# Layer 1's last stage in a four-layer graph network: four chunks' attention on ScalarE, the last softmax inside an output, scatters in five and three, x in twos

## The chip, the core and the metric

The kernel runs on one core of a Trainium2 chip. The core has five engines that work side by side, each with its own queue: TensorE (PE) for matrix products, VectorE (DVE), ScalarE (ACT), GpSimd (POOL), and SyncE (SP), which here only starts transfers. The metric is the device time of one launch in microseconds (us). The time before is 2069.36 us, the median of three runs (2069.28 to 2069.97).

## The reference

The input x has 128 x 64 = 8192 tokens of 256 numbers. Four layers follow each other, each of the form "normalize, cut off below zero, apply a graph network, add to x":

```python
h = jnp.maximum(_layernorm(x, axis=-1), 0.0)
x = x + _L1_gnn_ref(h, W_lin, W_val, a, W_out, adj, src, dst)
```

The change lies in layer 1, an attention over 512 edges of a graph with 64 nodes and 4 heads:

```python
Xq = (H @ W_lin.T).reshape(bt, n, h, dh);  Xv = (H @ W_val.T).reshape(bt, n, h, dh)
e = jnp.einsum('behd,hd->beh', leaky_relu(Xq[:, src] + Xq[:, dst], 0.2), a)
e = e + jnp.log(A0[src, dst] + EPS)[None, :, None]
# softmax of e over the edges with the same src gives attn
Y = segment_sum(attn[..., None] * Xv[:, dst], src)      # weighted sum of the values
return Y @ W_out.T
```

Layer 0 (products with the adjacency matrix and four LSTMs), layer 2 (two dense layers with batch norms) and layer 3 (a dense attention) are not touched. All numbers are 32-bit floats.

## The kernel before

**Chunks and groups.** Layer 1 works on 16 chunks of 512 tokens (NCH) and on 4 groups of 4 chunks. The edges of a group are scored together. Its softmax turns the scores into attention numbers for the 512 edges; these are scattered into a field in HBM that has a place for every pair of nodes (zero where there is no edge), and the field is read back as one dense tile `dense[g]` of 2 MB. From then on a chunk's weighted sum is a set of small dense products.

**A chunk's last steps.** `fetch(n)` (L1107) starts two transfers of 0.5 MB on SP: the values `xv` (chunks 12 to 15 still have theirs in SBUF) and the residual `x`, into a buffer of the pool `xo` (4 buffers), or, for chunks 13 to 15, into buffers that are no longer used. `turn_attention(n)` (L1126) copies the chunk's part of the dense tile into the order that PE needs, in two halves: `o = 0` on ACT, `o = 1` on DVE, both L1132, into a tile of the pool `attc` (3 buffers). `weigh(n)` (L1139) does the weighted sum: 32 small products, 64 matmul instructions in the trace (L1150), and a copy of the result to `yT` on ACT (L1160; 2 buffers). `put_out(n)` (L1165) multiplies by W_out in two halves of 8 matmul instructions each (L1171) and adds each half to x on DVE (L1181). Then x goes back to HBM (L1247 on SP), and `sums(n)` (L1185) takes mean and root of the variance for the next layer's norm: four pairs of `bn_stats` and `bn_aggr` on DVE (L1190, L1191), four small operations on POOL (L1193 to L1198). The tiles between DVE and POOL have 4 buffers.

**The order of a step.** `values_of(n)` (L1220) is a chunk's turn. It weighs chunk n, fetches chunk n + 2, turns the attention of chunk n + 2 (chunk 12, `LAST`, the first of the last group, is turned at the end of chunk 11's turn, and chunk 13 in chunk 12's), stores what was added a turn ago, puts out chunk n - 1, and then does some of the sums that are due. With `hold` the sums are put off. Chunks 0 to 3 have their turns between the edges of the last group; chunks 4 to 15 follow in the loop at L1328.

**The softmax of a group.** `edge_softmax(g)` (L1012) is a generator: each `yield` is a place at which other work is traced. `step_behind()` runs it to its next `yield`, `finish_behind()` to its end. It goes through an addition, four scans along the edges, a subtraction, an exponential on ACT (L1025), four reciprocals and a product that gives `e` (L1037), all but the exponential on DVE; then four transposes on PE (L1043), for the last group four scalings on ACT that give `attn` (L1051), eight indirect transfers from POOL (L1072, "scatters") and the read-back (L1093), which waits for all eight. POOL works its queue in order, so what is behind the read-back in it waits as well. For the last group (g = 3) the first four steps are taken after the last edges, the next seven in chunk 4's turn, the transposes and `attn` ahead of chunk 6's weighing. The scatters then go out in groups, each of which also waits for the last weighing traced before it (`last_weigh`, "weights first"):

```python
if len(sent) in (3, 6):
    yield
```

so three after chunk 6's weighing, three after chunk 7's, two and the read-back after chunk 8's.

**What sets the order on an engine.** A planner orders each engine's instructions by a simulation at build time. `late(ins)` pins an instruction behind the one that was traced before it on its engine; what has no pin can be moved forward past it. Pinned are the first matmul of a weighing and of an output, the copies L1132, the steps of the softmax, and (for the sums of chunk turns 8 to 10) the first POOL operation. Not pinned are the copies to `yT`, the additions L1181, all `bn_stats` and `bn_aggr`, and the transfers on SP. The dependencies themselves are kept by semaphores that the planner places.

## Time and profile before

| | |
|---|---|
| median of three runs | 2069.36 us |
| profiled execution, its own time | 2075.18 us |
| its span | 2073.3 us |
| mean granted PE clock | 0.992 |
| last group's edges end, chunk 3's weighing starts (PE) | 1606.83 us |
| chunk 4's weighing starts (PE) | 1611.57 us |
| last output of layer 1 ends (PE) | 1681.6 us |

Times within the span are microseconds from its start. The profiled execution is one more execution than the three that were timed, and its time is compared with profiled ones. In the profile a line "PE L1150 MATMUL pair<-att,xv_in 64*64 64x64 f32 x64" is a group of 64 instructions of source line 1150, with its start and its length ahead; in brackets stands how long the engine had been idle before it and what released it ("issue": nothing that the profile shows). "PEclk" is the share of its full clock that PE was granted, and the DMA share is the mean busy share of the core's 16 DMA engines. A line of the busy times by stretches gives the stretch, its length, the busy time and number of instructions of PE, of its weight loads, of DVE, ACT and POOL, then granted clock, DMA share and GB/s. In the waits, a line gives who waited for whom, the total in us, how often, and the longest.

### The profile page before, as it was taken

What the parts mean: (1) busy time and instruction counts of PE and PEld (TensorE: products, weight loads), DVE (VectorE), ACT (ScalarE), POOL (GpSimd) and SP (SyncE); (2) the same over time, 40 slices, a digit from 0 to 9 for tenths busy, and PEclk for the clock granted to TensorE, in tenths of its full rate; (3) what the DMA queues carried; (4) which work ended last, traced back from release to release, by engine and by line L of the source; (5) the groups of instructions that cost most, each with busy time, mean ns of one, the idle gap of its engine ahead of it and who ended that gap; (6) DMA issues with size and microseconds to landing.
All of it is one profiled execution on the core that took longest, in us unless ns stands there. A gap on an engine that the chain in (4) does not pass through costs nothing. (4 is left out here: it accounts for less than half of the span.)

```text
span 2073.3 us, 25490 instructions
## 1 busy us (share of the span) xinstructions
PE 2014.8 (97%) x9444; PEld 1353.1 (65%) x9444; DVE 1363.6 (66%) x2511; ACT 1183.8 (57%) x2226; POOL 306.0 (15%) x416
## 2 busy tenths in 40 slices
PE   8999999999999999999999999999999899999998
PEld 6777478766688855886667886333334775444786
DVE  8754666564665567567446556676776867886776
ACT  4344766554555467566456564666674456592544
POOL 3000010110100020002001001213322420000563
PEclk9999999999999999999999999999999999999899
DMA  9321000100100160001001003412223741022012
GB/s 315 96 97 51 0 21 1 41 0 1 41 1 1 64 220 21 1 1 41 1 0 41 1 16 132 143 51 97 75 83 137 260 173 51 0 75 88 31 62 72
DMA packets 63196, 135.06 MB, mean 65 GB/s; under 512 B 6240, under 2 KB 40928, under 8 KB 60768
## 3 DMA queue, kind: packets, MB, share of 16 engines
q1 hardware_dynamic: 56832, 109.11, 15.4%
q0 software_dynamic: 5632, 24.12, 3.2%
q8 instruction: 74, 1.21, 0.3%
q14 instruction: 50, 0.41, 0.1%
q10 hardware_dynamic: 608, 0.20, 0.1%
HBM read 87.28 MB, written 46.14 MB: 64 GB/s over the span
## 5 line engine op out<-in xcount | busy, mean ns | idle before, releaser
L651 PE MATMUL pa<-xop,sih 128*128 128x256 f32 (+2 forms) x1056 | 344.1, 418 | 11.4 <-DVE gate L705 7.7
L679 ACT ACTIVATE gate<-gate,bias 128x256 f32<-128x256 f32 (+2 forms) x368 | 248.3, 681 | 171.1 <-DVE gate L695 88.1
L651 PEld LDWEIGHTS pa<-xop,sih 128*128 128x128 f32 x1056 | 198.1, 190 | 87.2 <-issue 22.2
L651 PE MATMUL pc<-xop,wih 128*128 128x256 f32 (+2 forms) x736 | 251.1, 423 | 0.0
L695 DVE TENSOR_TENSOR gate<-pb,gate 128x256 f32<-128x256 f32 (+2 forms) x184 | 87.8, 477 | 225.0 <-PE pb L651 153.3
L651 PE MATMUL pa<-lstm_h,shh 128*128 128x256 f32 (+1 forms) x672 | 212.7, 398 | 0.0
L993 DVE SCALAR_TENSOR_TENSOR lr<-lr 128x1024 f32<-128x1024 f32 x128 | 151.7, 1227 | 55.0 <-ACT lr L992 55.0
L651 PEld LDWEIGHTS pc<-xop,wih 128*128 128x128 f32 x736 | 139.8, 190 | 51.2 <-issue 23.0
L710 DVE TENSOR_TENSOR gate<-pc,gate 128x256 f32<-128x256 f32 (+2 forms) x184 | 87.7, 477 | 120.8 <-PE pc L651 120.5
L992 ACT COPY lr<-pair 128x1024 f32<-128x1024 f32 x128 | 123.2, 1015 | 44.7 <-PE pair L986 43.8
L651 PEld LDWEIGHTS pa<-lstm_h,shh 128*128 128x128 f32 x672 | 127.7, 190 | 30.2
L651 PE MATMUL pc<-lstm_h,whh 128*128 128x256 f32 (+1 forms) x448 | 141.8, 398 | 0.0
L694 ACT COPY gate<-pa 128x256 f32<-128x256 f32 (+2 forms) x184 | 76.1, 414 | 97.1 <-PE pa L651 96.8
L986 PE MATMUL pair<-sd_hot,xq 64*128 64x512 f32 x512 | 127.8, 616 | 0.4 <-ACT lr L992 0.3
L705 DVE TENSOR_TENSOR gate<-pa,gate 128x256 f32<-128x256 f32 (+2 forms) x184 | 87.6, 476 | 43.9 <-PE pa L651 43.3
L970 PE MATMUL bank<-wlv,hT 128*128 128x512 f32 x240 | 110.7, 604 | 0.0
L699 ACT COPY gate<-pa 128x256 f32<-128x256 f32 (+2 forms) x184 | 75.6, 411 | 58.5 <-PE pa L651 57.2
L679 ACT ACTIVATE gate<-pa,bias 128x256 f32<-128x256 f32 (+2 forms) x184 | 94.3, 512 | 23.8 <-PE pa L651 22.2
L651 PE MATMUL pa<-xop,wih 128*128 128x256 f32 (+1 forms) x320 | 101.4, 398 | 2.7 <-ACT xop L632 2.7
L440 POOL TENSOR_TENSOR sih<-wih 128x512 f32<-128x512 f32 x8 | 10.2, 1270 | 631.8 <-DMA wih<-in_WihT 342.7
L651 PE MATMUL pb<-xop,wih 128*128 128x256 f32 (+1 forms) x320 | 100.3, 398 | 0.4 <-DVE gate L695 0.4
L651 PEld LDWEIGHTS pc<-lstm_h,whh 128*128 128x128 f32 x448 | 85.1, 190 | 20.1
(344 smaller groups left out, 3826.2 us busy)
## 6 DMA issues: line engine op xcount, KB each, us to landing
field<-sd_hot SPq DMA_DIRECT2D x4, 2304.0 KB, 17.6
wih<-in_WihT SPq DMA_DIRECT2D x8, 1024.0 KB, 4.9
xres<-in_x SPq DMA_DIRECT2D x16, 512.0 KB, 4.7
xa<-xres POOLq DMA_DIRECT2D x16, 512.0 KB
dense<-field POOLq DMA_DIRECT2D x4, 2048.0 KB
xin<-xb SPq DMA_DIRECT2D x16, 512.0 KB, 3.3
h<-xb SPq DMA_DIRECT2D x16, 512.0 KB, 3.2
xin<-in_x SPq DMA_DIRECT2D x15, 512.0 KB, 5.8
```

Of the source, the lines that this page charges most:

```text
L440: nc.gpsimd.tensor_tensor(o, x, y, op)
L651: ins = nc.tensor.matmul(p[:, : self.N], weights[kind, self.phase](k, q), x[k], start=first_ and kind == "ih", stop=kind == "hh" or not se ...
L679: nc.scalar.activation(out, in_, AF.Tanh if q == 2 else AF.Sigmoid, bias=bias[:, self.w - 1, 2 * q + j : 2 * q + j + 1],)
L694: nc.scalar.copy(blk[0, 0], pa[:, :N])
L695: nc.vector.tensor_tensor(blk[0, 0], pb[:, :N], blk[0, 0], ALU.add)
L699: nc.scalar.copy(blk[1, 0], pa[:, :N])
L705: nc.vector.tensor_tensor(blk[1, 1], pa[:, :N], blk[1, 1], ALU.add)
L710: nc.vector.tensor_tensor(blk[1, 0], pc[:, :N], blk[1, 0], ALU.add)
L970: ins = nc.tensor.matmul(p, hTs[n][:, k, i * P : (i + 1) * P], wlv[:, k, :], start=k == 0, stop=k == 1)
L986: ins = nc.tensor.matmul(p[:, par, :], queries[it][r, c * P : (c + 1) * P], sd_hot[r, :], start=True, stop=True)
L992: nc.scalar.copy(lr, p)
L993: nc.vector.scalar_tensor_tensor(lr, lr, 0.2, lr, ALU.mult, ALU.max)
```

## The change

Five things change in layer 1's last stage.

- **Attention on ACT.** For chunks 5, 6, 7 and 12, `turn_attention` makes both halves on ACT.
- **The last softmax's end.** `put_out` can do one half alone. In chunk 5's turn, output 4 is split: its first half, then the transposes and `attn`, then chunk 6's weighing, then its second half, whose first matmul has no pin.
- **Scatters.** Five after chunk 6's weighing, three and the read-back after chunk 7's.
- **x.** `fetch` starts the transfer of x only for chunks 0 to 5 and 12 to 15. Those of chunks 6 to 11 start in twos at the end of the turns of chunks 4, 5 and 6, into buffers of the pool `lrp` (6 buffers), which the edges no longer use.
- **Sums.** They are held up to chunk 6's turn instead of chunk 7's, so each pair of chunks comes a turn earlier. For the turns 7 to 10 the first `bn_stats` is pinned too, beside the first POOL operation.

```diff
--- before.py
+++ after.py
@@ -1086,7 +1086,7 @@
                             mybir.DependencyInfo(mybir.DependencyClass.Sync, mybir.DependencyReason.DATA),
                             reason="weights first",
                         )
-                        if len(sent) in (3, 6):
+                        if len(sent) == 5:
                             yield
                     elif ec % 2:
                         yield
@@ -1111,17 +1111,25 @@
             else:
                 xv = vp.tile([P, 4, D], F32, tag="xv", name="xv_in")
                 nc.sync.dma_start(out=xv, in_=xv_mem[n])
-            if n < NCH - 3:
+            fetched[n] = xv
+            if n < 6 or n >= LAST:
+                fetch_x1(n)
+
+        def fetch_x1(n):
+
+            if n < 6 or n == LAST:
                 xt = later_pools["xo"].tile([P, 4, D], F32, tag="xo", name="xo")
             else:
 
-                if n < NCH - 1:
+                if n < LAST:
+                    t = lrp.tile([P, 2, E], F32, tag="lr", name="xo_late")
+                elif n < NCH - 1:
                     t = t1.tile([P, 2, CHUNK], F32, tag="hT1", name="xo_last")
                 else:
                     t = w1.tile([P, 2, 2 * D], F32, tag="wlv", name="xo_last")
                 xt = t.rearrange("p c t -> p (c t)").rearrange("p (i d) -> p i d", d=D)
             nc.sync.dma_start(out=xt, in_=xa[n])
-            fetched[n] = (xv, xt)
+            fetched_x[n] = xt
 
         def turn_attention(n):
 
@@ -1129,7 +1137,7 @@
             att = later_pools["attc"].tile([P, 2, 8, T], F32, tag="att", name="att")
             for o in range(2):
                 late(
-                    (nc.vector.tensor_copy if o else nc.scalar.copy)(
+                    (nc.vector.tensor_copy if o and n not in (5, 6, 7, LAST) else nc.scalar.copy)(
                         att[:, o, :, :],
                         dense[g][:, :, o * 32 + m * 8 : o * 32 + m * 8 + 8].rearrange("p s r -> p r s"),
                     )
@@ -1138,7 +1146,7 @@
 
         def weigh(n):
 
-            (xv, xt), att = fetched.pop(n), turned.pop(n)
+            xv, att = fetched.pop(n), turned.pop(n)
             yT = yp.tile([P, 8, 2, T], F32, tag="yT", name="yT")
             p = pair_bank()
             for c in range(2):
@@ -1160,11 +1168,12 @@
             nc.scalar.copy(
                 yT.rearrange("p k o t -> p o k t"), p.rearrange("p o (k t) -> p o k t", t=T)
             )
-            return xt, yT
-
-        def put_out(n, xt, yT):
-
-            for b in range(2):
+            return (yT,)
+
+        def put_out(n, yT, halves=(0, 1)):
+
+            xt = fetched_x[n]
+            for b in halves:
                 p = bank()
                 for i in (2 * b, 2 * b + 1):
                     for c in range(2):
@@ -1179,15 +1188,18 @@
                             late(ins)
                 x2 = xt[:, 2 * b : 2 * b + 2, :].rearrange("p i d -> p (i d)")
                 nc.vector.tensor_tensor(x2, p, x2, ALU.add)
-            stores.append((n, xt))
-            unnormed.append((n, xt))
+            if halves[-1]:
+                stores.append((n, xt))
+                unnormed.append((n, xt))
 
         def sums(n, xt, keep=False):
 
             st = stat.tile([P, 4, 6], F32, tag="ln_st", name="ln_st")
             mv = stat.tile([P, 4, 2], F32, tag="ln_mv", name="ln_mv")
             for i in range(4):
-                nc.vector.bn_stats(st[:, i, :], xt[:, i, :])
+                ins = nc.vector.bn_stats(st[:, i, :], xt[:, i, :])
+                if keep and i == 0:
+                    late(ins)
                 nc.vector.bn_aggr(mv[:, i, :], st[:, i, :])
             rs, nm = w12t["x_rs"][:, n, :], w12t["x_nm"][:, n, :]
             ins = nc.gpsimd.tensor_scalar(rs, mv[:, :, 1], 1e-5, None, ALU.add)
@@ -1214,15 +1226,17 @@
 
         NT = NTOK // P
         last_weigh = [None]
+        fetched_x = {}
         dense, fetched, turned, weighed, stores, unnormed = {}, {}, {}, [], [], []
         LAST = NCH - 4
 
         def values_of(n, hold=False):
 
             one = (n, *weigh(n))
-            if n in (6, 7):
+            if n == 6:
                 step_behind()
-            elif n == 8:
+                put_out(*split.pop(), (1,))
+            elif n == 7:
                 finish_behind()
             if n + 2 < NCH:
                 fetch(n + 2)
@@ -1231,7 +1245,13 @@
             if n + 2 < NCH and not LAST <= n + 2 < LAST + 2:
                 turn_attention(n + 2)
             flush_stores()
-            flush_values()
+            if n == 5:
+
+                split.extend(weighed)
+                put_out(*weighed.pop(), (0,))
+                step_behind()
+            else:
+                flush_values()
 
             if n + 1 == LAST:
                 turn_attention(LAST)
@@ -1239,7 +1259,7 @@
             if not hold:
                 for _ in range(2 if n > 6 else 4):
                     if unnormed:
-                        sums(*unnormed.pop(0), 8 <= n < 11)
+                        sums(*unnormed.pop(0), 7 <= n < 11)
 
         def flush_stores():
             while stores:
@@ -1249,6 +1269,8 @@
         def flush_values():
             if weighed:
                 put_out(*weighed.pop())
+
+        split = []
 
         def next_score():
             q, c, lrs = waiting.pop(0)
@@ -1329,9 +1351,10 @@
             if n == 4:
                 for _ in range(7):
                     step_behind()
-            if n == 6:
-                step_behind()
-            values_of(n, 4 <= n < 8)
+            values_of(n, 4 <= n < 7)
+            if n < 7:
+                for k in (2 * n - 2, 2 * n - 1):
+                    fetch_x1(k)
             if n - 10 in first_x2:
                 scale_x(n - 10, first_x2.pop(n - 10))
         flush_stores()
```

## The prediction

> **What bounds the kernel now.** I read the page first, then busy time by stretches of 10 us through layer 1's last stage, then each engine's timeline there, and last the waits by length. The page says that TensorE (PE) is the bound:
>
> ```profile
> PE 2014.8 (97%) x9444; PEld 1353.1 (65%) x9444; DVE 1363.6 (66%) x2511; ACT 1183.8 (57%) x2226; POOL 306.0 (15%) x416
> ```
>
> What can be won is the time in which PE idles or runs at a lower clock. The stretches find it in the stage that the change touches:
>
> ```profile
> 1640.00:1650.00 10.00, 10.00 (x164) 8.42 (x163) 3.80 (x17) 4.89 (x7) 8.62 (x18) 1.00 0.99 346
> 1650.00:1660.00 10.00, 5.51 (x77) 4.48 (x76) 7.84 (x25) 4.52 (x7) 8.78 (x17) 0.78 0.61 192
> 1660.00:1670.00 10.00, 10.00 (x159) 8.17 (x158) 6.58 (x19) 3.49 (x4) 4.15 (x11) 0.88 0.45 178
> ```
>
> PE is full up to 1650, then busy 5.51 of 10 us, and for two stretches the granted clock (the number after POOL's) is 0.78 and 0.88. PE's timeline shows why:
>
> ```profile
> 1626.43 0.96 PE L1150 MATMUL pair<-att,xv_in 64*64 64x64 f32 x41
> 1627.85 0.62 PE L1150 MATMUL pair<-att,xv_in 64*64 64x64 f32 x23 [0.46 <-issue]
> ...
> 1632.05 1.01 PE L1150 MATMUL pair<-att,xv_in 64*64 64x64 f32 x44
> 1633.44 0.59 PE L1150 MATMUL pair<-att,xv_in 64*64 64x64 f32 x20 [0.37 <-issue]
> ...
> 1647.09 1.16 PE L1150 MATMUL pair<-att,xv_in 64*64 64x64 f32 x64
> ...
> 1651.84 0.34 PE L1150 MATMUL pair<-att,xv 64*64 64x64 f32 x8
> 1656.67 1.77 PE L1150 MATMUL pair<-att,xv 64*64 64x64 f32 x56 [4.49 <-DVE att L1132]
> 1658.38 5.72 PE L1171 MATMUL bank<-wout,yT 128*128 128x256 f32 x16
> 1664.03 1.16 PE L1150 MATMUL pair<-att,xv 64*64 64x64 f32 x64
> ```
>
> L1150 is a chunk's weighing (64 matmuls), L1171 its output (16). Undisturbed, a chunk takes 4.74 us (chunk 10, from 1642.35 to 1647.09). From chunk 11 (1647.09) to chunk 13 (1664.03) it is 16.94 instead of 9.48: **7.46 us lost at chunk 12**. Its first 8 matmuls run, the rest wait 4.49 us for a copy of its attention on VectorE (DVE); then 56 matmuls take 1.77 us instead of 1.02 (64 take 1.16) and the output 5.72 instead of 3.72: 2.75 us of slow clock. A second loss is smaller: chunks 7 and 8 take 5.62 and 5.56 us, 0.88 + 0.82 = 1.70 us over, with gaps after 41 and 44 matmuls that no engine's semaphore explains ("issue"). GpSimd (POOL), ScalarE (ACT) and DVE show what stands behind both:
>
> ```profile
> 1623.65 1.11 POOL L1072 DMA_INDIRECT field<-attn,row_of  x1 [27.12 <-ACT attn L1051]
> ...
> 1636.04 0.96 POOL L1072 DMA_INDIRECT field<-attn,row_of  x1 [0.30 <-issue]
> 1640.56 0.60 POOL L1093 DMA_DIRECT2D dense<-field  x1 [3.56 <-DMA field<-attn,row_of]
> ```
> ```profile
> 1650.31 1.10 ACT L1132 COPY att<-dense 128x512 f32<-128x512 f32 x1 [0.92 <-DVE ln_mv L1191]
> ```
> ```profile
> 1655.46 0.66 DVE L1181 TENSOR_TENSOR xo<-bank,xo 128x512 f32<-128x512 f32 x1
> 1656.03 0.58 DVE L1132 COPY att<-dense 128x512 f32<-128x512 f32 x1
> ```
> ```profile
> DVE ln_mv L1191 <- POOL x_nm L1197: 5.2, 3, 2.6
> ```
>
> The last softmax's eight scatters (L1072) go out in 3, 3 and 2, each group after the weighing of chunk 6, 7, 8; the read-back of the dense attention (L1093) starts at 1640.56. It has landed by 1650.31, when ACT copies chunk 12's first half (the releaser named there is no input of that copy). The second half on DVE stands behind the additions of chunk 10 in DVE's order and starts only at 1656.03. DVE is late because its aggregations waited 5.2 us for POOL, which itself stood behind the read-back until 1640.56. So the wait that ends last at chunk 12 is DVE's queue, not the transfer.
>
> [...] 0.50 granted from 1656 to 1662 after 4.49 us idle, full again at 1664. [...] here the share is 0.99 while the read-back runs (1640 to 1650).
>
> **The change part by part.**
>
> *Attention of chunks 5, 6, 7 and 12 all on ACT.* Four copies leave DVE (0.56 to 0.62 us each, 2.4 in all) and cost ACT 1.08 each, 4.3. For 5 to 7 ACT idles 1.85 to 2.74 us per chunk there and PE wants them a chunk later: nothing on the path. For chunk 12 the copy leaves the late DVE queue. ACT's copy of chunk 11's yT starts 0.20 after its weighing, takes 0.91 to the next start, then come 2 x 1.08: 3.3 us, against the 3.65 us of output 10 that PE has first. **0.35 us to spare, if the read-back has landed.** The 4.49 us wait goes, and with it the slow clock: 7.46.
>
> *The transposes of the last softmax between two halves of output 4, chunk 6's weighing after them.* They move from 1621.13 to 1617.41 + 1.86 = 1619.27. Needed by then: the product e, finished on DVE at 1620.98. In front of it on DVE stood chunk 5's copy (0.53 of its time) and statistics of about 1.6 us which the new pin on each first bn_stats may keep out. So e is ready between 1618.9 and 1620.5, and PE waits 0 to 1.3 us, unless the planner fills the wait with output 4's second half, which has no pin; I take 0.5. Its transposes then let ACT make attn, but only after chunk 7's two copies: 1618.51 + 2 x 1.08 = 1620.7, plus 1.15 = 1621.8, against 1622.95 before: 1.1 us earlier. Output 4's second half and the later release of its yT lie before chunk 7's needs.
>
> *Scatters in five and three.* Before, the first scatter started 0.7 us after attn, and they follow each other by 1.27 to 1.42. So the five run from 1622.5 to about 1628.7 and now reach past chunk 7's weighing at 1626.43 or later. Before, PE went on 0.4 us after a group's last scatter (1627.46 to 1627.85, 1632.99 to 1633.44). At 1628.7 that ends chunk 7's weighing at about 1629.0 instead of 1628.47: **a loss of 0.5 us**, which swallows the 0.5 of the transposes, since it ends with the scatters, not with PE. The bound above: the third softmax's scatters ran under all of chunk 2's weighing, which took 4.57 instead of 1.09 and left the clock at 0.5 (output 5.14 instead of 3.72), 4.9 us; below: 0.88 saved. The three then follow 0.76 after the weighing, at 1629.8 to 1633.5, and meet chunk 8 as before (0.82, unchanged).
>
> *The read-back.* It waits 1.9 (third softmax) to 3.56 us (here) after the last scatter: 1635.4 to 1637.1, 3.5 to 5 us earlier. It took at most 9.1 us from its issue's end under a DMA share of 0.99; so it lands by 1646.8, three us before ACT can use it (1649.4 + 0.5).
>
> *x fetched in twos.* x of chunks 6 to 11 goes into buffers free since 1606.8 (the last scores), issued at chunks 4, 5 and 6; before, each waited on SP for a store of four chunks earlier. Six transfers of 0.5 MB move from 1616 to 1653 to about 1612 to 1625, where the share was 0.55 to 0.61. On SP they stand ahead of xv of chunks 7 and 8, wanted at 1626 and 1632: 2 MB ahead at 346 GB/s are 6 us, so chunk 8's, issued at 1617.5 before and 3.8 us under way, lands by 1627.3. The 4.7 us up to 1632 hide it; what went beyond them would cost PE in full. I cost it at nothing.
>
> *Sums from chunk 7, pinned.* The same instructions in another order. Chunks 7 to 10 now carry two sums each on DVE: 2 x 1.8, additions 1.35, a copy 0.55, 5.5 us against 4.74. Counted from the last addition of output 6 (1631.8) DVE does nine sums (16.2), four outputs (5.4) and two copies (1.1) by 1654.5, so chunk 13's copy, which stands behind sums 10, ends at 1655.1. PE wants it at about 1656.8: **1.7 us to spare**. POOL starts its sums at about 1636.5, 2.06 each plus 2.9 for w2S, and releases DVE's buffers four sums ahead (sums 6 by 1650), before DVE asks.
>
> Sum: -7.46 + 0.5 = -6.96. What comes after (the first sums of layer 2, with 1.29 us of waiting for ACT at 1685.4) moves with PE unchanged. The profiled execution took 2075.18 us with a span of 2073.3 and so lies 5.8 us over the median 2069.36. I take the difference over: 2068.2 profiled, 2062.4 at the median.
>
> **The rivals.** *A, DVE late at chunk 13.* The pin holds only the first of four bn_stats, and POOL still starts behind the read-back. If DVE again waits 5.2 us for POOL, chunk 13's copy is 5.2 - 1.7 = 3.5 us late, with half of the clock's 2.75 us: gain 7.0 - 4.9 = 2.1, **2067.3**. For it: DVE's 5.5 us per chunk against PE's 4.74. Against: POOL is free 4 us sooner. *B, DVE becomes the bound from chunk 8 on.* All of sums 2 to 9 now stand in front of the copies of chunks 10, 11 and 13, where some were done in earlier gaps. If the wait for POOL doubles to 10.4, PE idles 8.7 us at chunk 13, with 2.75 of slow clock: 11.4 - 7.0 is 4.4 lost, **2073.8**. It decides from a delay of DVE of 1.7 + 7.0 - 2.75 = 6 us. Against it: DVE is relieved of 2.4 us of copies. *C, the issue gaps shrink too*[...]: 1.7 more than the 7.46, **2060.2**. Against it: three of three scatter groups that met a weighing delayed it. *D, the edit doesn't do what it says:* the order on an engine comes from a planner wherever an instruction isn't pinned; an ACT order with yT of chunk 6 before attn would start the scatters 2 us later. That costs about 2 and stays in the forecast's range.
>
> **How the numbers follow.** Forecast (with D) 0.55, A 0.22, B 0.15, C 0.08. The likeliest is 2062.4, its own range 2061 to 2065 (the fetch from 0.88 saved to twice the loss taken, D's 2 us; its worst, 4.9, gives 2066.8). About 0.2% (4.1 us) is what the measurement tells from no change. Faster: the forecast, C, and the mild end of A, 0.67; same: the rest of A, 0.18; slower: B, 0.15. The range reaches from C to the far side of A, 2059.8 to 2069.5, and leaves B out.
>
> **What would show it.** Right: no PE wait over 1 us at chunk 12, clock 1.00 from 1650 to 1670, chunk 13 near 1657, the read-back issued before 1638, ACT's two copies of chunk 12 back to back. Wrong: PE waiting on DVE's attention copy at chunk 13 (A, B), on dense at chunk 12 (read-back not early), or a clock of 0.5 after chunk 7 (scatters).

## The result, and the profile after

| | before | after |
|---|---|---|
| median, us | 2069.66 (8 runs, 2067.67 to 2072.82) | 2061.84 (8 runs, 2060.79 to 2064.53) |
| ratio, 95% interval | | 0.9963 (0.9952 to 0.9974) |
| profiled execution, us | 2075.18 | 2061.03 |
| its span, us | 2073.3 | 2059.3 |
| mean granted PE clock | 0.992 | 0.996 |

The change takes 7.8 us off the median; from the interval of the ratio, 5.4 to 9.9. The two profiled executions lie 14.2 us apart, nearly twice as much, so the first thing to settle is which part of that difference belongs to the change. Line numbers after: the attention copies are L1140 (before L1132), a weighing L1158 (L1150), the copy to `yT` L1168 (L1160), an output L1180 (L1171), the additions L1190 (L1181), `bn_stats` and `bn_aggr` L1200 and L1203 (L1190, L1191), POOL's sums L1205 to L1210 (L1193 to L1198). L1072, L1093 and L1043 have not moved.

The page's first part, after:

```profile
PE 2006.1 (97%) x9444; PEld 1346.1 (65%) x9444; DVE 1359.5 (66%) x2507; ACT 1184.4 (58%) x2230; POOL 308.2 (15%) x416
```

PE's busy time fell from 2014.8 to 2006.1 us with the same 9444 instructions. At chunk 12 this is the clock coming back, not work left out: its output took 5.72 us before, with a granted clock of 0.50 from 1656 to 1662, and takes 3.72 after. Not all of it is the change's: the profile before also had a lower clock at chunk 2 (0.91 from 1580 to 1600; after 1.00) and in later layers (0.91 from 1810 to 1830, after 1.00 from 1800 to 1830; 0.83 from 1900 to 1940, after 0.87). The stretches of 10 us (same columns as before) that answer to those shown for the kernel before:

```profile
1640.00:1650.00 10.00, 10.00 (x165) 8.40 (x164) 9.50 (x34) 8.24 (x13) 8.52 (x19) 1.00 0.49 197
1650.00:1660.00 10.00, 10.00 (x164) 8.43 (x163) 7.62 (x23) 3.78 (x4) 6.87 (x17) 1.00 0.27 107
1660.00:1670.00 10.00, 10.00 (x112) 8.75 (x111) 8.38 (x26) 1.17 (x2) 3.39 (x8) 1.00 0.77 273
```

PE is busy for all 30 us and the granted clock, 0.78 and 0.88 before, is 1.00 throughout. PE's timeline in the same stage:

```profile
1602.11 1.16 PE L1158 MATMUL pair<-att,xv_in 64*64 64x64 f32 x64
...
1615.62 0.63 PE L1043 MATMUL bank<-ident,e 128*128 128x128 f32 x4 [0.94 <-DVE e L1037]
...
1622.65 1.16 PE L1158 MATMUL pair<-att,xv_in 64*64 64x64 f32 x64
...
1627.39 1.22 PE L1158 MATMUL pair<-att,xv_in 64*64 64x64 f32 x64
...
1641.68 1.16 PE L1158 MATMUL pair<-att,xv_in 64*64 64x64 f32 x64
...
1646.42 1.16 PE L1158 MATMUL pair<-att,xv 64*64 64x64 f32 x64
...
1651.16 1.16 PE L1158 MATMUL pair<-att,xv 64*64 64x64 f32 x64
...
1668.75 3.78 PE L50 MATMUL bank<-bdH,h 128*128 128x128 f32 x32
```

Chunks 11, 12 and 13 start 4.74 us apart: the wait at chunk 12 is gone. The weighings of chunks 7 (1622.65) and 8 (1627.39) run through without a gap. One wait is new: the transposes of the last softmax, now between the halves of output 4, stand 0.94 us for `e` on DVE. POOL, ACT and DVE, in that order:

```profile
1618.14 1.11 POOL L1072 DMA_INDIRECT field<-attn,row_of  x1 [21.61 <-ACT attn L1051]
...
1627.62 0.96 POOL L1072 DMA_INDIRECT field<-attn,row_of  x1 [0.30 <-issue]
1632.12 0.59 POOL L1093 DMA_DIRECT2D dense<-field  x1 [3.53 <-DMA field<-attn,row_of]
```
```profile
1643.87 2.07 ACT L1140 COPY att<-dense 128x512 f32<-128x512 f32 x2
```
```profile
1641.32 0.18 DVE L1203 BATCH_NORM_AGGREGATE ln_mv<-ln_st 128x2 f32<-128x6 f32 x1 [0.35 <-POOL x_nm L1209]
...
1648.35 1.10 DVE L1140 COPY att<-dense 128x512 f32<-128x512 f32 x2
```

All eight scatters follow each other, because chunk 7's weighing, for which the last three wait, ended before POOL came to them. The read-back starts at 1632.12, 30.0 us after chunk 3's weighing (1602.11), where it had been 33.7 (1640.56 less 1606.83). ACT's two copies for chunk 12 start behind chunk 11's `yT` without waiting for the dense tile. DVE waits 0.35 us for POOL instead of 5.2, and its copy for chunk 13 starts at 1648.35, 2.8 us before PE wants it.

**A measure that holds.** From the first matmul of layer 2's sums (L50 in PE's timeline) to the end of the span the profiles have 391.7 us before and 390.6 after; 0.8 of the 1.1 us is a wait in layer 2 that both kernels have and that ended in half clock in one of the two profiles (two matmuls behind it in 2.07 us before, in 1.13 after; "A layer 2 tile earlier", below). Up to chunk 3's weighing they differ, but that part also differs between executions of one kernel: a second profile of the kernel before comes to it at 1601.53 instead of 1606.83. So the length of the stage itself, from chunk 3's weighing to the first L50, is what the experiments are read by: 74.78 us before (1606.83 to 1681.61), **66.64 after** (1602.11 to 1668.75). In the profile before the two ends are:

```profile
1606.83 1.16 PE L1150 MATMUL pair<-att,xv_in 64*64 64x64 f32 x64
...
1681.61 3.78 PE L50 MATMUL bank<-bdH,h 128*128 128x128 f32 x32
```

### The profile page after: what moved, and what is told of

It is laid out like the page before. It is cut to its first block, busy times and chain, and to the rows that moved or that the text cites. A ratio compares the mean times of both kernels' runs of the same rounds, so it can differ in the third digit from the quotient of the medians.

```text
span 2059.3 us, 25491 instructions
## 1 busy us (share of the span) xinstructions
PE 2006.1 (97%) x9444; PEld 1346.1 (65%) x9444; DVE 1359.5 (66%) x2507; ACT 1184.4 (58%) x2230; POOL 308.2 (15%) x416
## 5 line engine op out<-in xcount | busy, mean ns | idle before, releaser
L651 PE MATMUL pa<-xop,sih 128*128 128x256 f32 (+2 forms) x1056 | 344.4, 418 | 11.7 <-DVE gate L705 8.2
```

The source lines that it names most:

```text
L651: ins = nc.tensor.matmul(p[:, : self.N], weights[kind, self.phase](k, q), x[k], start=first_ and kind == "ih", stop=kind == "hh" or not se ...
```

## The experiments

Kernels that were to be compared ran on one chip, beside the kernel before. "Stage" is read from one profile each, and one execution can stand far from the median: those of b_act12 took 2061.04 to 2069.11 us, and the profiled execution of a_332 (2063.79 us) was the fastest of its twelve. So the stage says where time went in that execution, and the medians say what an edit is worth.

| run | base and edit | stage, us | median, us | ratio to before, 95% interval |
|---|---|---|---|---|
| b_again | before, profiled again | 74.01 | 2069.22 (one run) | |
| b_act12 | before, chunk 12 on ACT | 69.99 | 2066.08 | 0.9986 (0.9979 to 0.9994) |
| b_act12_53 | the same, scatters 5 and 3 | 68.86 | 2063.83 | 0.9982 (0.9973 to 0.9991) |
| a_dve12 | after, chunk 12's half back on DVE | 68.11 | 2061.73 | 0.9971 (0.9960 to 0.9982) |
| a_332 | after, scatters 3, 3, 2 | 71.21 | 2068.11 | 0.9999 (0.9990 to 1.0007) |
| a_x_single | after, x one by one | 66.63 | 2061.07 | 0.9966 (0.9954 to 0.9979) |
| a_no_pin | after, no `bn_stats` pinned | 66.84 | 2061.03 | 0.9960 (0.9944 to 0.9975) |
| a_all_pins | after, all four pinned | 69.73 | 2062.95 | 0.9975 (0.9966 to 0.9984) |
| a_no_split | after, output 4 whole | 66.08 | 2060.03 | 0.9962 (0.9950 to 0.9974) |
| a_no_split_no_pin | after, both undone | 68.02 | 2062.32 | 0.9971 (0.9959 to 0.9983) |
| a_no_split_no_pin_h | the same, a layer 2 tile earlier | 67.96 | 2060.06 | 0.9965 (0.9956 to 0.9974) |
| a_no_split_h | a_no_split, that tile earlier | 70.55 | 2069.81 | 0.9974 (0.9967 to 0.9981) |

Beside them the kernel before had medians of 2068.19, 2068.76, 2068.28 and, beside a_no_split_h, 2075.39 us. So that row is read against its own 2075.39 alone. The changed kernel itself did not run beside them; on the first of these chips a_x_single stands for it.

**The kernel before once more.** Nothing is edited; the question is what of its profile recurs.

> The kernel before once more, for a second profile. If the issue gaps of the first profile (chunk 2's weighing 4.57 us with the slow clock after it, chunks 7 and 8 0.88 and 0.82 us over) belong to that one execution: none of them here, the stage from chunk 3's weighing to the first sums of layer 2 takes 73.1 instead of 74.8 us, and the wait at chunk 12 stays near 7.5 us. If scatters that meet a weighing always hold up PE's instructions, as I argued: chunk 2 again near 4.6 us, and 0.8 to 0.9 over at chunks 7 and 8.

PE's timeline of this second profile:

```profile
1640.12 1.16 PE L1150 MATMUL pair<-att,xv_in 64*64 64x64 f32 x64
...
1646.96 0.34 PE L1150 MATMUL pair<-att,xv 64*64 64x64 f32 x8 [2.02 <-ACT att L1132]
1650.33 1.77 PE L1150 MATMUL pair<-att,xv 64*64 64x64 f32 x56 [3.03 <-DVE att L1132]
...
1657.95 1.16 PE L1150 MATMUL pair<-att,xv 64*64 64x64 f32 x64
```

and ACT's:

```profile
1645.85 1.06 ACT L1132 COPY att<-dense 128x512 f32<-128x512 f32 x1 [3.43 <-DMA dense<-field]
```

No weighing has a gap here, chunk 2's included, although the scatters ran beside the same ones. What remains is chunk 12, and there are *two* waits. The first 8 matmuls stand 2.02 us for ACT's half, whose copy began at 1645.85 after ACT had idled 3.43 us for the read-back. The other 56 then stand 3.03 us for DVE's half, and the slow clock follows. From chunk 11 to chunk 13 it is 17.83 us, 8.35 more than 2 x 4.74. In the first profile the gaps at chunks 7 and 8 had put PE 1.7 us further back within the stage, and the read-back had landed at most 9.8 us after its start (1640.56 to 1650.31) instead of 11.7, so that only the second wait showed.

**Chunk 12's half on ACT, alone.**

```diff
--- before.py
-                    (nc.vector.tensor_copy if o else nc.scalar.copy)(
+                    (nc.vector.tensor_copy if o and n != LAST else nc.scalar.copy)(
```

> The kernel before with one edit: both halves of chunk 12's attention are copied on ScalarE. Theory Q (the loss at chunk 12 was VectorE's queue, not the transfer): the dense tile has landed by 1650.3, two copies of 1.08 us end at 1652.5, chunk 12's matmuls go on there instead of at 1656.67, with no slow clock: 6.5 to 7.4 us faster than before. Rival T (the loss needs the earlier read-back, that is the scatters and x): the second copy finds the same wait a little later, less than 2 us faster.

```profile
1648.94 0.34 PE L1150 MATMUL pair<-att,xv 64*64 64x64 f32 x8 [1.94 <-ACT att L1132]
1649.91 1.77 PE L1150 MATMUL pair<-att,xv 64*64 64x64 f32 x56 [0.63 <-ACT att L1132]
...
1655.99 1.16 PE L1150 MATMUL pair<-att,xv 64*64 64x64 f32 x64
```

DVE's wait is gone, the read-back's is not: 1.94 us, then 0.63 for the second of ACT's two copies, and 56 matmuls still take 1.77 us. Of the 8.35 us the stage gains 4.02 (74.01 to 69.99); the timed gain is 2.1 us by the medians, 2.9 by the ratio. Theory Q's 6.5 to 7.4 us are missed: it overlooked the read-back's own wait. Rival T's "less than 2 us" is a little low.

**The same half back on DVE, in the changed kernel.**

```diff
--- after.py
-                    (nc.vector.tensor_copy if o and n not in (5, 6, 7, LAST) else nc.scalar.copy)(
+                    (nc.vector.tensor_copy if o and n not in (5, 6, 7) else nc.scalar.copy)(
```

> The changed kernel with chunk 12's second half back on VectorE, all else kept. Theory Q: the copy stands behind the additions of output 10 (the last one ends at 1647.4 in the changed kernel) and ends at about 1648, 1.5 us after PE wants it at 1646.5[...], so 1 to 2 us slower than the changed kernel. Rival T: no difference, since the read-back stays early. Rival Q2 (the copy on VectorE is the whole loss whatever the backlog): 7 us slower.

```profile
1645.84 1.04 PE L1158 MATMUL pair<-att,xv 64*64 64x64 f32 x56 [1.24 <-DVE att L1140]
```

PE waits 1.24 us for DVE and keeps its full clock (56 matmuls in 1.04 us); the stage is 1.47 us longer. That is the 1 to 2 us of theory Q: with DVE no longer held up by POOL, this copy's place costs 1.5 us, where it cost 3.03 and the slow clock in b_again. The timed difference (2061.73 to 2061.07 for a_x_single beside it) is too small to tell. Read the other way round, this run is the change *without* the copy that the prediction gave its whole 7.46 us to: it still takes the stage from 74.01 to 68.11, 5.90 of the 7.37 us. The copy alone brought 4.02 (b_act12). The two overlap, and a reason is at hand: an earlier read-back also lets POOL's sums start earlier, for which DVE waits 5.8 us in b_again and 0.35 here.

**Scatters in 3, 3 and 2 again.**

```diff
--- after.py
-                        if len(sent) == 5:
+                        if len(sent) in (3, 6):
...
             elif n == 7:
+                step_behind()
+            elif n == 8:
                 finish_behind()
```

> The changed kernel with the scatters in three, three and two again, the last two and the read-back after chunk 8's weighing. Theory Q: the read-back is issued about 3 us later and lands by about 1644.5, still before ScalarE can copy chunk 12 (1643.9), so 0 to 1 us slower than the changed kernel; GpSimd's sums start 3 us later and VectorE waits a little longer. Rival T: the read-back ends last again, 3 us and the slow clock, 4 to 7 us slower.

The stage is 4.57 us longer, where theory Q had 0 to 1. By the median (2068.11, a_x_single beside it 2061.07) the whole gain is gone, 7.0 us; the profile, of its fastest execution, accounts for 4.57 of them, and where the rest goes is not shown. POOL's timeline and PE's show the 4.57:

```profile
1626.74 0.23 POOL L1205 TENSOR_SCALAR x_rs<-ln_mv 128x4 f32<-128x4 f32 x1 [0.95 <-DVE ln_mv L1203]
...
1629.28 1.08 POOL L1072 DMA_INDIRECT field<-attn,row_of  x1 [0.18 <-issue]
...
1635.67 0.67 POOL L1093 DMA_DIRECT2D dense<-field  x1 [1.73 <-DMA field<-attn,row_of]
```
```profile
1646.33 0.34 PE L1158 MATMUL pair<-att,xv 64*64 64x64 f32 x8 [2.19 <-ACT att L1140]
1647.30 1.77 PE L1158 MATMUL pair<-att,xv 64*64 64x64 f32 x56 [0.62 <-ACT att L1140]
```

The edit does more than it names. The last two scatters are now traced behind the first pinned sums (L1205), so in POOL's queue they stand behind them (1626.74), and the read-back starts 35.8 us into the stage (1635.67 less 1599.83) instead of 30.0. Chunk 12 then waits 2.19 and 0.62 us for it and runs on at half clock (56 matmuls in 1.77 us; 0.50 granted from 1648 to 1650). So this is no price of the grouping by itself; it is the price of a read-back 5.8 us late, with POOL's first sums moved ahead of it and the rest as in the changed kernel.

**Chunk 12 on ACT and scatters in 5 and 3, nothing else.** Do these two lines make the change?

```diff
--- before.py
-                    (nc.vector.tensor_copy if o else nc.scalar.copy)(
+                    (nc.vector.tensor_copy if o and n != LAST else nc.scalar.copy)(
...
-                        if len(sent) in (3, 6):
+                        if len(sent) == 5:
...
-            if n in (6, 7):
+            if n == 6:
                 step_behind()
-            elif n == 8:
+            elif n == 7:
                 finish_behind()
```

> The kernel before with two edits alone: both halves of chunk 12 on ScalarE, and the scatters in five and three with the read-back after chunk 7's weighing. Not the split output, not x in twos, not the three other copies, not the earlier pinned sums. Theory S (two waits in series at chunk 12, the read-back and behind it VectorE's queue; one edit takes each, the rest is worth nothing): no wait over 1 us at chunk 12, the stage from chunk 3's weighing to layer 2's first sums takes 65.7 to 67 us (74.0 in the second profile of the kernel before, 66.6 in the changed kernel), 6 to 8 us faster than before. Rival R (the rest of the change makes the scatters land early): a wait on ScalarE's copy of 1.5 us or more with the slow clock, stage 68 us or more.

```profile
1635.67 0.60 POOL L1093 DMA_DIRECT2D dense<-field  x1 [5.61 <-DMA field<-attn,row_of]
```
```profile
1643.59 3.80 PE L1171 MATMUL bank<-wout,yT 128*128 128x256 f32 x16 [0.78 <-DVE xo L1181]
...
1648.74 0.34 PE L1150 MATMUL pair<-att,xv 64*64 64x64 f32 x8 [1.35 <-ACT att L1132]
1649.71 1.04 PE L1150 MATMUL pair<-att,xv 64*64 64x64 f32 x56 [0.63 <-ACT att L1132]
```
```profile
1647.62 2.04 ACT L1132 COPY att<-dense 128x512 f32<-128x512 f32 x2 [3.67 <-DMA dense<-field]
```

No; theory S's 65.7 to 67 us are missed. Rival R's 68 us or more are there, but its signs only in part: it wanted a wait of 1.5 us or more and the slow clock. The scatters now follow each other as after, but when the last has been issued the read-back waits 5.61 us for them to land, where the changed kernel waits 3.53. It starts 32.6 us into the stage (after: 30.0), DVE behind POOL is late for a bank (0.78), and chunk 12 waits 1.35 and 0.63. The clock stays full (56 matmuls in 1.04 us), and 68.86 lies between. The traffic differs: from 1622 to 1632 the DMA share is 0.90 here and 0.72 after. Here x of chunks 7 and 8 is issued on SP at 1622.78 and 1625.39, amid the scatters; after, all six x transfers are issued by 1610.

That the traffic delays the scatters doesn't hold by itself, though. The run a_no_split_no_pin below has all six x transfers as early as the changed kernel, and its scatters land as late as here. What it has instead is a faster read-back:

```profile
1634.44 0.59 POOL L1093 DMA_DIRECT2D dense<-field  x1 [5.96 <-DMA field<-attn,row_of]
```
```profile
1643.35 2.07 ACT L1140 COPY att<-dense 128x512 f32<-128x512 f32 x2 [1.24 <-DMA dense<-field]
```

It takes 8.91 us from its issue to ACT's copy, and PE, 1.37 us late by a wait for a bank, doesn't wait at chunk 12; here it takes 11.95 us. So a read-back slower by 3 us stands behind the wait here. That the traffic slows it is not shown: no run changes it alone, and in the first profile of the kernel before the read-back had landed within 9.8 us at a share of 0.99.

**x one by one, in the same other buffers.**

```diff
--- after.py
-            if n < 6 or n >= LAST:
-                fetch_x1(n)
+            fetch_x1(n)
...
-            if n < 7:
-                for k in (2 * n - 2, 2 * n - 1):
-                    fetch_x1(k)
```

> The changed kernel with x of chunks 6 to 11 fetched one by one with the values, in their old places of the order, still into the edges' buffers. My prediction costed the twos at nothing: within 0.7 us of the changed kernel. Rival (the earlier x is what makes scatters and read-back land earlier): read-back 2 us or more later, and 2 us or more slower.

Stage 66.63 us, that is 0.01 off. On SP the six x transfers are issued from 1599 to 1610 in both kernels, before chunk 5's weighing starts (1611.59 in the changed kernel) and not at the ends of the turns in which they are written: they have no pin, their buffers are free, and the planner moves them to the same place wherever they are written. The twos do nothing. The other buffers, which let all six go so early, may do something, through the traffic just named; they were not tried by themselves, since the sums, which come a turn earlier, would then hold the old ones.

**The pins.** Without any, then on all four `bn_stats` of a chunk:

```diff
--- after.py
-                if keep and i == 0:
+                if False:
```

> The changed kernel without the pin on the first bn_stats. More statistics go ahead of e on VectorE: the transposes wait 0.4 to 1 us longer than 0.94, and 0.3 to 1 us slower. Rival (the pin keeps VectorE from becoming the bound): attention copies late at chunks 8 to 13, 3 us slower or more.

```diff
--- after.py
-                if keep and i == 0:
+                if keep:
```

> The changed kernel with all four bn_stats of the sums of turns 7 to 10 pinned, not only the first. The transposes' 0.94 us wait for e in the changed kernel comes from three bn_stats that the planner still moved ahead of e on VectorE: the wait goes, chunk 6 is weighed 0.9 us earlier. VectorE then has about 1.5 us more to do later; its copy for chunk 13 had 2.2 us to spare, so 0.3 to 0.9 us faster than the changed kernel in all. Rival A (VectorE late at chunk 13): a wait there of 1 us or more, same or slower.

Without pins the stage is 66.84 us, 0.2 longer (0.3 to 1 expected), with 1.20 us of waiting at the transposes. With all four, where 0.3 to 0.9 us less were expected, the wait at the transposes is gone, since no statistics can come ahead of `e` any more, and the stage is 3.09 us longer (2062.95 us by the median, 2061.03 without pins beside it):

```profile
1648.15 0.34 PE L1158 MATMUL pair<-att,xv 64*64 64x64 f32 x8
1650.57 1.04 PE L1158 MATMUL pair<-att,xv 64*64 64x64 f32 x56 [2.08 <-DVE att L1140]
1651.55 5.38 PE L1180 MATMUL bank<-wout,yT 128*128 128x256 f32 x16
```

The statistics that could no longer be done early in DVE's free time now stand before chunk 13's copy, which PE awaits for 2.08 us; the output after it takes 5.38 us instead of 3.72. This is a wait at rival A's place, but not for rival A's reason: the trace has no wait of DVE for POOL in this stage. It is its own work in another order.

**Output 4 whole.** The transposes come after it, before chunk 6's weighing:

```diff
--- after.py
-                put_out(*split.pop(), (1,))
...
-            if n == 5:
-
-                split.extend(weighed)
-                put_out(*weighed.pop(), (0,))
-                step_behind()
-            else:
-                flush_values()
+            flush_values()
...
+            if n == 6:
+                step_behind()
             values_of(n, 4 <= n < 7)
```

> The changed kernel with output 4 whole and the transposes and attn ahead of chunk 6's weighing, as before. The 0.94 us wait for e goes; the scatters start about 0.7 us later, and the read-back with them. If it had 1.6 us to spare at chunk 12 (theory: the split is worth nothing): 0.5 to 0.9 us faster than the changed kernel. Rival T (the read-back ends last as soon as it is later): a wait on ScalarE's copy at chunk 12 and 0.5 to 3 us slower.

PE no longer waits for `e`. The read-back starts 31.9 us into the stage, 1.9 later than after, because it waits 5.27 us for the scatters' landing; it is still early enough to cost nothing. DVE's copy for chunk 13 is a little late instead:

```profile
1649.75 1.04 PE L1158 MATMUL pair<-att,xv 64*64 64x64 f32 x56 [0.35 <-DVE att L1140]
```

Net 0.56 us shorter in this profile: the split gains nothing by itself, it costs a little. The medians can't tell the two apart (ratios 0.9962 and 0.9963). Then the pin is taken out as well:

```diff
--- after.py (beside the edit above)
-                if keep and i == 0:
+                if False:
```

> The changed kernel with output 4 whole (transposes and attn ahead of chunk 6's weighing) and without the pin on the first bn_stats. The wait of 0.94 us for e goes (0.62 us to spare without the split, 0.26 used by the missing pin), VectorE's copy for chunk 13 comes earlier than with the pin, so no wait there: stage 65.6 to 66 us, 0.6 to 1 us faster than the changed kernel. Rival (the pin is needed against VectorE's backlog): a wait at chunk 13 of 0.35 us or more as without the split, stage 66.1 us or more.

```profile
1642.34 3.79 PE L1180 MATMUL bank<-wout,yT 128*128 128x256 f32 x16 [1.37 <-DVE xo_late L1190]
...
1651.98 1.04 PE L1158 MATMUL pair<-att,xv 64*64 64x64 f32 x56 [0.82 <-DVE att L1140]
```

Two waits on DVE, 1.37 us for a bank and 0.82 for chunk 13's copy, and 68.02 us instead of the 65.6 to 66 expected. Each of the two parts can go alone at 0.2 us or at a small gain; without both, DVE is late. It waits 9.2 us for POOL here (0.35 in the changed kernel), whose sums stand behind a read-back that starts 33.0 us into the stage. Whether the missing pin makes the scatters land so late is not shown.

**A layer 2 tile earlier.** The changed kernel and the one before both have a wait of 1.28 us for ACT in the first sums of layer 2. Here the third normed tile gets a buffer of its own and is made ahead of the step it stood behind, first in a_no_split_no_pin, then in a_no_split:

```diff
--- after.py (beside the edits above)
-            h2[n] = hpool.tile([P, 4, D], F32, tag="h", name="h")
+            h2[n] = (hpool if n != 2 else own_h[0]).tile([P, 4, D], F32, tag="h", name="h")
...
-                aggregated(0)
                 scale_x(2, coming2.pop(2))
+                aggregated(0)
```

> The kernel above, and chunk 2's normed tile of layer 2 made by ScalarE before the copies of the first sums, into a buffer of its own. PE's 1.28 us wait for ScalarE at the third sums goes: 1 to 1.3 us faster than the kernel above, 1.6 to 2.3 us faster than the changed kernel. Rival (the x of chunk 2 is not back from HBM when ScalarE comes to it, and the copies behind it wait): same or slower.

> The changed kernel with output 4 whole again (transposes after it and before chunk 6's weighing) and with the third normed tile of layer 2's first sums made earlier, in a buffer of its own; the pins stay. Theory: the two edits act at different places and add up. The stage from chunk 3's weighing to layer 2's first sums stays at 66.1 us (66.08 with the whole output 4 alone, 66.64 in the changed kernel), no wait over 0.5 us at chunks 12 and 13, full clock, and the wait of 1.28 us in the first sums of layer 2 is gone: about 1.8 us under the changed kernel, near 2060.0. Rival: the copy that is moved ahead on ScalarE delays the yT or attention copies of the last chunks, so that the 1.28 us come back as a wait at chunks 14 or 15 or at the second sums: the same time as with the whole output 4 alone.

The wait is gone in both (48 matmuls L50 run in one piece, 5.62 us), and the end comes no sooner: from the first L50 to the end of the span it is 390.7 and 391.1 us, against 390.6 in the changed kernel. Layer 2 is 1.1 us ahead for some 135 us and then loses 0.8 of it at a wait that both have, and the rest later. PE's timeline of the changed kernel and of a_no_split_no_pin_h there:

```profile
1806.62 1.13 PE L1428 MATMUL pa<-h,w2T 128*128 128x512 f32 x2 [1.85 <-ACT h L1545]
1807.58 1.02 PE L1428 MATMUL pb<-h,w2T 128*128 128x512 f32 x2
1809.20 1.99 PE L1428 MATMUL pa<-tri,w2S 128*128 128x512 f32 x4 [0.60 <-ACT h L1447]
```
```profile
1806.84 1.90 PE L1425 MATMUL pa<-h,w2T 128*128 128x512 f32 x2 [1.85 <-ACT h L1543]
1808.53 1.92 PE L1425 MATMUL pb<-h,w2T 128*128 128x512 f32 x2
1810.23 2.00 PE L1425 MATMUL pa<-tri,w2S 128*128 128x512 f32 x4
```

The same 1.85 us of idleness is followed by full clock (1.13 and 1.02 us) in one and by half clock (1.90 and 1.92) in the other; a wait of 0.60 falls away behind it. a_no_split_h does the same (1.71 and 1.91), but so do three profiles without this edit, both of the kernel before and that of b_act12_53. This is no effect of the edit, then; what decides it is not shown. So the expectation of a_no_split_h has the 1.28 us wait right and the gain from it wrong, and no version is shown to beat the changed kernel: 2060.03 and 2060.06 us are below 2061.84, with intervals of the ratio that overlap.

The last run brought something else. Its PE timeline, at chunk 2 and at chunk 7:

```profile
1578.74 0.36 PE L1158 MATMUL pair<-att,xv_in 64*64 64x64 f32 x4 [0.39 <-issue]
...
1623.73 1.12 PE L1158 MATMUL pair<-att,xv_in 64*64 64x64 f32 x45
1625.29 0.27 PE L1158 MATMUL pair<-att,xv_in 64*64 64x64 f32 x2 [0.43 <-issue]
1626.70 0.34 PE L1158 MATMUL pair<-att,xv_in 64*64 64x64 f32 x4 [1.15 <-issue]
...
1628.77 4.88 PE L1180 MATMUL bank<-wout,yT 128*128 128x256 f32 x16
```

The "issue" gaps of the first profile are back, on the chip on which the kernel before took 2075.39 us; the run is still 5.6 us below that. Chunk 2's weighing takes 4.68 us (1.09 undisturbed, start to next start), chunk 7's 5.04, and output 6 behind it is slowed from 3.65 to 4.82. Without these 5.1 us at chunk 7 the stage would be 65.4 us. Of fourteen profiles two have such gaps of over 0.25 us between 1560 and 1700 us, and in both they stand only within or at the end of weighings beside which scatters are under way. In the other twelve the scatters run beside weighings too, and there are none. The packed traces also hold transfers of the kind "instruction". In the first profile of the kernel before, one of 16 KB falls on the first two gaps at chunk 2 (1580.84 to 1582.07), but none on the gaps at chunks 7 and 8, and in the changed kernel's profile one of 1.64 us beside the scatters (1624.21) goes with no gap. So what makes the gaps is not shown.

## Why the prediction was right, step by step

The predicted time, 2062.4 us, is 0.6 us off, and the predicted gain, 7.0, lies inside the measured 5.4 to 9.9. Not every term is right, and that the sum came so near is in part luck: the main term was 0.9 us too small, the cost against it 0.4 too small, and the main term was credited to one edit where two share it.

- **Chunk 12's wait and slow clock, -7.46.** The wait and the slow clock went, as forecast. The size, without gaps, is 8.35, and the reading behind it was incomplete: "the wait that ends last at chunk 12 is DVE's queue, not the transfer" is true, but removing it alone uncovers the transfer. b_act12 has only that half and gains 4.0 of the stage's 8.35; the change without that half (a_dve12) keeps 5.9 of its 7.4; a late read-back in the changed kernel (a_332) gives 4.6 back. The prediction counted the early read-back as something that must merely not come in the way ("three us before ACT can use it"). It is at least as much a part of the gain as the copy.
- **Transposes, 0 to 1.3, 0.5 taken.** 0.94: three unpinned `bn_stats` still went ahead of `e`. The term was too small by 0.44. The sum without gaps is then -8.35 + 0.94 = -7.41, and the stages differ by 7.37 (74.01 to 66.64).
- **"A loss of 0.5 us" at chunk 7 and 0.82 kept at chunk 8.** (In the prediction's range of 2061 to 2065 this term is "the fetch".) This step failed. In the changed kernel's profile both weighings run through, and before's second profile has no gaps to keep. What one execution showed was taken for a cost of every execution. That the gaps meet only weighings beside scatters has held in both profiles that have any; their cause is not shown. The bound of 4.9 us for a group of scatters over a weighing was no idle one: chunk 7 in a_no_split_h lost 5.1.
- **The 5.8 us between the profiled execution and the median.** For the median it was right to leave them out, since they belonged to that one execution. For the next profile it was wrong to expect them again: 2068.2 was forecast and 2061.03 came. They have a place now: the second profile of the kernel before is 5.3 us earlier at chunk 3's weighing, which is chunk 2's gaps (5.2 us), and 0.8 shorter in the stage.
- **First scatter and read-back.** The first scatter was put at 1622.5, 15.7 us into the stage; it came at 16.0. The read-back was put at 28.6 to 30.3 us; it came at 30.0. That it lands "at most 9.1 us from its issue's end" is no bound, though: b_act12_53 took 11.35 to ACT's copy.
- **ACT at chunk 12, 0.35 us to spare.** The second copy ended at 1645.94 for a weighing at 1646.42: 0.48.
- **DVE at chunk 13, 1.7 us to spare.** The first of the two copies that start at 1648.35 (1.10 us together) ended near 1648.9 for 1651.16: 2.3. DVE waited 0.35 us for POOL. A wait at rival A's place appears once the statistics are pinned more tightly (a_all_pins: 2.08 us), so it was a near one, though there it isn't POOL that delays DVE. In the changed kernel rival B did not come about: nothing near twice 5.2 us of waiting for POOL.
- **x in twos, nothing.** For the twos this is right, though not for the reason given: they are not even a change of order. That x goes so much earlier in its new buffers was costed at nothing too; what that is worth was not tried, and b_act12_53 leaves room for a gain.
- **Rival C.** By its sign, no loss at chunks 7 and 8, it came true for the profile after. As a saving of 1.7 us over the median before it did not: the profile of before at 2069.22 us had no gaps to save.

What stays open: why the gaps come in some executions and not in others, why the read-back waits 3.5 us for the scatters in the changed kernel and 5.3 with output 4 whole, with the same x traffic; and how much of the last 2.2 us between b_act12_53 and the changed kernel is x, how much the other copies and the sums.

## What to carry to other kernels

When an operand is late, look at all its inputs, not at the one that comes last: here a copy in a slow queue stood 3 us behind a transfer that was 2 us late itself. What each part brings alone doesn't add up then: 4.0 us for the copy, 5.9 for the change without it, 7.4 for both. Profile the kernel before twice before a loss is read from it, and compare stages inside the profiles, since a loss that only one execution has can hide another that all have. Look also at what stands behind a wait in the same queue: before, POOL idled 3.56 us for the scatters until the read-back at 1640.56 and began its sums right behind it, at 1641.23. The earlier read-back (1632.12 after, the sums from 1632.79) mattered to them too, and through their buffers to DVE.

## What the runs showed of the hardware

- **The length of a wait alone didn't say whether the clock drops.** At chunk 12, 1.24 us idle (a_dve12) and 1.35 with 0.63 (b_act12_53) left it full, with the 56 matmuls behind in 1.04 us. At chunks 12 and 13, 1.94 with 0.63 (b_act12), 2.19 with 0.62 (a_332) and 2.08 (a_all_pins) were followed by half clock and cost PE a further 1.5 to 1.7 us. The wait of 1.85 us in layer 2, after the same earlier waits, left it full in nine of the fourteen profiles (the two matmuls behind it in 1.12 or 1.13 us) and halved it in five (1.71 to 2.07). So waits of about 2 us came out on either side here, and the gain of removing one can include clock; what decides it is not shown.
- **What half clock cost at chunk 12.** The 56 matmuls and the output behind them took 1.77 and 5.72 us in the first profile of the kernel before, 1.77 and 5.99 in its second (b_again), 1.77 and 4.45 in b_act12, 1.77 and 4.53 in a_332; in a_dve12, at full clock, 1.04 and 3.72.
- **Gaps without a releaser come and go.** Within layer 1's last stages they are absent from twelve profiles and cost about 6.9 us in one (5.2 from chunk 2's weighing to the projections behind it, 1.7 at chunks 7 and 8) and 10.4 in another (5.3 and 5.1).
- **The landing of the same eight scatters** came 3.44 us after the end of the last one's issue in a_all_pins and 5.96 in a_no_split_no_pin. **The read-back of 2 MB**, where ACT waited for it, took 8.91 us from its issue to ACT's copy in a_no_split_no_pin and 11.95 in b_act12_53. What makes the difference is not shown.
